# Trainium2, one core: first layernorm's halves abreast, bias shifts summed on VectorE first, norm steps timed by single matmuls, last image's MLP and convolution by token halves

## The chip, the cores and the metric

One NeuronCore of a Trainium2 chip runs the whole program in one launch. The metric is the device time in microseconds (us), the median over several executions. Times of stages come from one profiled execution of each kernel, whose span is about 2 us shorter than the timed median.

## The reference, cut to what matters

Eight images of 384 channels and 32 x 32 tokens pass a transformer block, then a ConvNeXt-like block. All arithmetic is fp32.

```python
# block 1, per image; C = 384, N = 1024 tokens, 8 heads of 48
xn = layernorm(x, g1, beta1)                       # eps 1e-5
q, k, v = xn @ w_qkv.T + b_qkv
x1 = softmax(q k^T * SCALE) v @ w_proj.T + b_proj + x
x2 = x1 + gelu(layernorm(x1, g2, beta2) @ w_fc1.T + b_fc1) @ w_fc2.T + b_fc2   # hidden 1536
# block 2, per image
y = depthwise_conv_7x7(x2) + dw_b                  # one filter per channel, padding 3
y = gelu(layernorm(y, ln_w, ln_b) @ w1 + b1)       # eps 1e-6, hidden 1536
gx = sqrt(sum over tokens of y^2);  nx = gx / (mean over hidden of gx + 1e-6)
y = (gamma * y * nx + gbeta + y) @ w2 + b2
out = x2 + y
```

Below, fc1 and fc2 are the two matmuls of block 1's MLP; the GRN (global response normalization) is the scaling by `nx` in block 2, with the up-projection `w1` before it and the down-projection `w2` after it. A norm's additive vector (`beta1`, `beta2`, `ln_b`, `gbeta`) is folded once into the bias of the matmul behind it: that is a bias shift. The kernel calls the last two shifts lnb and gbeta.

## The kernel before: the parts that the change touches

Activations lie with channels on the 128 partitions (3 channel tiles, `CT`) and tokens along the free dimension, in two halves of 512 (`NH`). TensorE multiplies; VectorE does the 7 x 7 convolution as 147 fused multiply-adds per image over a padded copy; ScalarE does exponentials and GELU; GpSimd does the layernorm's additions and copies rows into the padded image. While TensorE works on image b's attention and MLP, VectorE convolves image b-1.

In the traces each engine executes its instructions in the order in which the program emits them (in the changed kernel VectorE's first subtraction, whose sum was ready at 10.4 us, stands behind two additions and starts at 14.2), so the program decides where a layernorm's matmul stands among the MLP's matmuls. It does this with an emission clock: `flow.pe(us)` advances it by the TensorE time of what was just emitted, and background chains (generators) take their next step when the clock passes the delay that they yielded.

```python
U = 0.857                       # us of one 128x128 by 512 fp32 matmul

class Flow:
    def pe(self, us):           # TensorE work was emitted: step the chains that are due
        self.now += us
        ...
        while self.due and self.due[0][0] <= self.now:
            at, _, chain, paced = heapq.heappop(self.due)
            self._step(chain, at, paced)
    ...
def shift(dst, lhsT, name, nk, bias, rows=slice(0, P)):   # bias + W^T beta, one column
    ps = o_tile(f"shift_{name}")
    for k in range(nk):
        nc.tensor.matmul(out=ps[rows, :1], lhsT=lhsT(k), rhs=col(name, k), start=(k == 0), stop=(k == nk - 1))
    nc.vector.tensor_tensor(dst, ps[rows, :1], bias, ALU.add)

def linear_half(lhsT, rhs, nk, h, name):
    ps = o_tile(name)
    for k in range(nk):
        nc.tensor.matmul(out=ps, lhsT=lhsT(k), rhs=rhs(k)[:, half(h)], start=(k == 0), stop=(k == nk - 1))
    flow.pe(nk * U)             # the clock ticks once per tile
    return ps

def layernorm(src, dst, h, eps, g, name, switch):
    cols = half(h)
    a = one.tile([P, NH], F32, tag="ln_a", name=f"{name}_a{h}")
    nc.gpsimd.tensor_tensor(a, src[:, 0, cols], src[:, 1, cols], ALU.add)
    nc.gpsimd.tensor_tensor(a, a, src[:, 2, cols], ALU.add)
    yield 3.5
    total = o_tile(f"{name}_sum{h}")
    nc.tensor.matmul(out=total, lhsT=ones, rhs=a, start=True, stop=True)
    flow.pe(U)
    yield 1.0
    for ct in range(CT):        # x - mean
        nc.vector.scalar_tensor_tensor(dst[:, ct, cols], total, -1.0 / C, src[:, ct, cols], ALU.mult, ALU.add)
    yield 0.8
    ...                         # three squares on ScalarE, "yield 0.7" after each
    nc.gpsimd.tensor_tensor(squares[0], squares[0], squares[1], ALU.add)
    nc.gpsimd.tensor_tensor(squares[0], squares[0], squares[2], ALU.add)
    yield 3.5
    var = o_tile(f"{name}_var{h}")
    nc.tensor.matmul(out=var, lhsT=ones, rhs=squares[0], start=True, stop=True)
    flow.pe(U)
    yield 1.0
    ...                         # rstd = exp(-0.5 ln(var + eps)) on ScalarE
    yield 2.6 if switch else 1.2
    for ct in range(CT):
        nc.vector.scalar_tensor_tensor(dst[:, ct, cols], dst[:, ct, cols], col(g, ct), rstd, ALU.mult, ALU.mult)

def both(*args):                # one half after the other
    for h in range(2):
        yield from layernorm(*args[:2], h, *args[2:])

def mlp(b, xt, xn, weights, tag, ln, rest, before_fc2, fold):
    ...
    flow.finish(ln)             # the second norm, half 0
    for m in range(HT):         # fc1 on half 0: 12 tiles of 3 matmuls
        if fold and m + 2 < HT:
            fold_fc1(weights, wa, m + 2)          # a shift
        gelu_half(hid, m, 0, xn, weights, wa, bfc1, f"fc1_{b}")
        if m == 3 and rest:
            rest()              # second half of the output projection
            ln = flow.spawn(layernorm(xt, xn, 1, eps0, "g2", f"ln2_{b}", True))
    flow.finish(ln)             # whatever of half 1's norm is not emitted yet comes here
    for m in range(HT):
        gelu_half(hid, m, 1, xn, weights, wa, bfc1, f"fc1_{b}")
        weights.used(wa, m)
    if before_fc2:
        before_fc2()            # spawns the norms of the image before and the image after
    for ct in range(CT):        # fc2 on both halves, then x += ..., copied into the padded image
        ...

def convolution(acc, us):       # us: paced emission
    for i in range(KS * KS):
        dy, dx = divmod(i, KS)
        for ct in range(CT):
            window = pad[:, ct, dy : dy + H, dx : dx + W]
            dst = image(acc[:, ct, :])
            ...
            nc.vector.scalar_tensor_tensor(dst, window, tap, dst, ALU.mult, ALU.add)
            yield us

# main, end of the run
for b in range(B):
    ...
    mlp(b, xt, xn, weights, b, ln2, rest, norms, b == 0)
    ...
    if b == B - 1:
        start_conv(b, "xn", 1.3)                  # the last convolution: only after the last MLP
    y, gx = grn_up(b - 1, acc, weights, b - 1, b == 1)
    ...
    scale = flow.spawn(grn_scale(b - 1, gx, weights, b - 1, b == 1))
    next_values(b + 1)
    flow.finish(scale)
    grn_down(b - 1, y, kept.pop(b - 1), weights, b - 1, b - 1)
flow.finish(state["conv"])
acc = state["acc"]
flow.finish(both(acc, acc, eps1, "lnw", f"ln3_{B - 1}", True))
y, gx = grn_up(B - 1, acc, weights, B - 1, False)
...
```

## Time and profile before

| | before |
|---|---|
| time, median of the first 3 runs | 3819.84 us (3818.61 to 3821.57) |
| span of the profiled run | 3816.7 us |
| TensorE busy, idle | 3660.0 us, 157 us |
| first query matmul | 62.9 us |
| second output projection of the last image starts | 3325.1 us |
| from there to the end | 491.6 us |

TensorE's own time line at the start (start us, length us, engine, line, operation, out<-in, tile, count) shows what the first part of the change is after: 60 matmuls of one column each (120 records), for the bias shifts, stand between the first norm and the values.

```profile
25.28 2.07 PE L281 MATMUL ln_var<-ln_sq,ones 128*128 128x512 f32 x2 [5.59 <-POOL ln_sq L278]
27.15 10.24 PE L200 MATMUL shift_beta<-vec,wqk_sb 128*128 128x1 f32 x48
37.31 2.26 PE L200 MATMUL shift_beta<-vec,wv_sb 128*48 128x1 f32 x48
39.51 5.28 PE L652 MATMUL bout<-bv,wproj_sb 128*128 128x1 f32 x24
44.65 18.43 PE L319 MATMUL v<-wv_sb,xn 128*128 128x384 f32 x48
```

The bracket names what the engine waited for just before, 5.59 us for GpSimd's sum of squares. A record count is twice the number of matmuls that the program wrote.

### The profile page before, as it was taken

The page shows a single profiled execution, that of the slowest core. Times are in us where ns is not written, and L with a number is a line of the kernel's source. Part 1 is how long each engine was busy: PE and PEld are TensorE (multiplying, and loading weights), DVE is VectorE, ACT ScalarE, POOL GpSimd, SP SyncE. Part 2 cuts the span into 40 slices and gives each one's busy share as a digit, 9 for nine tenths or more (in the row PEclk, how much of TensorE's full clock was granted, in tenths as well). Part 3 has the DMA queues.
Part 4 walks back from the last instruction along what each step waited for, and adds up shares of the span by engine and source line. Part 5 has one row for each costly group of instructions (what it writes and reads, how often), then busy time and mean ns, then how long its engine had stood idle before and what let it go on. Part 6 is the DMA issues. An engine that isn't in the chain of part 4 may idle for free.

```text
span 3816.7 us, 36079 instructions
## 1 busy us (share of the span) xinstructions
PE 3660.0 (96%) x14882; PEld 1620.2 (42%) x14882; DVE 1862.4 (49%) x1931; ACT 1264.8 (33%) x1523; POOL 433.9 (11%) x294
## 2 busy tenths in 40 slices
PE   8999999999999999999999999999999999999658
PEld 4354444454444434444344443444444443444223
DVE  1011785246732668227571366524673256826930
ACT  1541352313523144240542415322352314423021
POOL 1011021200112002110021001120021200210010
PEclk9999999999999999999999999999999999999879
DMA  2002101201012200121002210021101210002100
GB/s 103 13 12 58 45 18 45 70 29 45 18 45 75 65 10 16 42 88 52 13 12 62 68 53 16 25 88 36 45 18 44 75 57 19 15 25 72 53 18 29
DMA packets 87148, 161.47 MB, mean 42 GB/s; under 512 B 25920, under 2 KB 26048, under 8 KB 86848
## 3 DMA queue, kind: packets, MB, share of 16 engines
q1 hardware_dynamic: 86400, 156.01, 13.6%
q8 instruction: 119, 1.95, 0.2%
q10 hardware_dynamic: 576, 3.07, 0.2%
q14 instruction: 53, 0.43, 0.0%
HBM read 133.36 MB, written 25.69 MB: 42 GB/s over the span
## 4 chain that ended last, share of the span: by engine, by line
PE 95%; DVE 2%; ACT 2%; POOL 1%; DMA 0%; issue 0%; DVEq 0%; SPq 0%; POOLq 0%; ACTq 0%
PE fc L250 13%; PE o L235 13%; PE h L235 13%; PE fc L235 13%; PE o L401 12%; PE s L381 11%; PE qk L235 9%; PE proj L333 4%; PE v L319 3%; DVE acc L538 2%; PE ln_sum L265 1%; PE ln_var L281 1%; ACT L255 1%; PE shift_beta L200 1%; PE shift_gbeta L200 0%; DMA xn<-in_x 0%
## 5 line engine op out<-in xcount | busy, mean ns | idle before, releaser
L538 DVE SCALAR_TENSOR_TENSOR acc<-pad,vec,acc 128x1024 f32<-128x1024 f32 x1152 | 1449.1, 1326 | 0.0
L390 ACT ACTIVATE p<-s 128x1024 f32<-128x1024 f32 x512 | 523.7, 1025 | 401.3 <-PE s L381 401.2
L381 PE MATMUL s<-qk 64*64 64x512 f32 x4096 | 563.1, 591 | 11.5 <-ACT p L390 10.0
L401 PE MATMUL o<-p,v 64*64 64x512 f32 x4096 | 560.9, 590 | 0.0
L250 PE MATMUL fc<-xn,fc 128*128 128x512 f32 x1152 | 515.7, 606 | 26.9 <-DVE xn L292 26.9
L235 PE MATMUL o<-y,w 128*128 128x512 f32 x1152 | 499.8, 596 | 3.2 <-issue 3.2
L235 PE MATMUL h<-acc,w 128*128 128x512 f32 x1152 | 502.3, 594 | 0.6 <-DVE acc L292 0.6
L235 PE MATMUL fc<-hid,fc 128*128 128x512 f32 x1152 | 502.4, 593 | 0.0
L250 PEld LDWEIGHTS fc<-xn,fc 128*128 128x128 f32 x1152 | 221.7, 194 | 310.5 <-issue 269.6
L235 PEld LDWEIGHTS o<-y,w 128*128 128x128 f32 x1152 | 220.2, 191 | 279.1 <-issue 273.3
L235 PEld LDWEIGHTS fc<-hid,fc 128*128 128x128 f32 x1152 | 219.2, 190 | 276.4 <-issue 276.4
L235 PEld LDWEIGHTS h<-acc,w 128*128 128x128 f32 x1152 | 218.2, 190 | 272.0 <-issue 269.4
L235 PE MATMUL qk<-xn,wqk_sb 128*128 128x512 f32 x768 | 330.9, 592 | 0.0
L368 POOL TENSOR_TENSOR attn<-attn,r 128x512 f32<-128x512 f32 x64 | 103.4, 1615 | 1897.2 <-DMA r<-back 1896.5
L381 PEld LDWEIGHTS s<-qk 64*64 64x64 f32 x4096 | 178.6, 133 | 279.3 <-issue 229.0
L401 PEld LDWEIGHTS o<-p,v 64*64 64x64 f32 x4096 | 185.3, 133 | 258.2 <-issue 252.6
L483 ACT ACTIVATE hid<-fc,bfc_f 128x512 f32<-128x512 f32 x192 | 132.0, 687 | 457.3 <-PE fc L250 457.3
L306 ACT ACTIVATE qk<-qk,bqk 128x1024 f32<-128x1024 f32 x64 | 71.3, 1114 | 634.2 <-PE qk L235 634.2
L350 DVE TENSOR_TENSOR attn<-o,attn 128x512 f32<-128x512 f32 x64 | 44.3, 691 | 396.5 <-ACT attn L348 396.1
L235 PEld LDWEIGHTS qk<-xn,wqk_sb 128*128 128x128 f32 x768 | 145.9, 190 | 183.3 <-issue 182.5
L552 ACT ACTIVATE y<-h,b_f 128x1024 f32<-128x1024 f32 x96 | 107.0, 1114 | 290.2 <-PE h L235 290.0
L269 DVE SCALAR_TENSOR_TENSOR acc<-ln_sum,acc 128x512 f32<-128x512 f32 x48 | 30.2, 684 | 283.7 <-PE ln_sum L265 283.7
(90 smaller groups left out, 1843.3 us busy)
## 6 DMA issues: line engine op xcount, KB each, us to landing
fc<-in_wfc SPq DMA_DIRECT2D x96, 384.0 KB
w<-in_w SPq DMA_DIRECT2D x96, 384.0 KB
r<-back SPq DMA_DIRECT2D x128, 128.0 KB
xn<-in_x SPq DMA_DIRECT2D x16, 768.0 KB
x<-in_x SPq DMA_DIRECT2D x16, 768.0 KB
kept<-x SPq DMA_DIRECT2D x8, 1536.0 KB
res<-kept SPq DMA_DIRECT2D x48, 256.0 KB
out_y<-res SPq DMA_DIRECT2D x48, 256.0 KB
```

The lines of the kernel that those rows point to most:

```text
L235: nc.tensor.matmul(out=ps[:, half(h)], lhsT=lhsT(k), rhs=rhs(k)[:, half(h)], start=(k == 0), stop=(k == nk - 1),)
L250: nc.tensor.matmul(out=ps, lhsT=lhsT(k), rhs=rhs(k)[:, half(h)], start=(k == 0), stop=(k == nk - 1))
L306: nc.scalar.activation(parts[:, i, :], ps, AF.Identity, bias=bqk[:, i : i + 1], scale=SCALE if i < NP else 1.0)
L319: nc.tensor.matmul(out=ps[:, :C], lhsT=xn[:, k, t * P : (t + 1) * P], rhs=wv_sb[:, k, :], start=(k == 0), stop=(k == CT - 1),)
L333: nc.tensor.matmul(out=ps, lhsT=wproj_sb[:, m, ct * P : (ct + 1) * P], rhs=attn[:, m, :], start=(m == 0), stop=(m == NP - 1),)
L368: nc.gpsimd.tensor_tensor(attn[:, m, :], attn[:, m, :], r, ALU.mult)
L381: nc.tensor.matmul(out=s[64 * i : 64 * i + 64, j, :], lhsT=kT[64 * j : 64 * j + 64, m, k0 : k0 + 64], rhs=qT[64 * j : 64 * j + 64, m, half ...
L390: nc.scalar.activation(p, s, AF.Exp)
L401: nc.tensor.matmul(out=outs[i][64 * j : 64 * j + 64, :], lhsT=v[keys, t, at : at + 64], rhs=p[keys, j, :], start=(t == 0), stop=(t == KT - 1),
L483: nc.scalar.activation(hid[:, m, half(h)], ps, AF.Gelu, bias=bias[:, m : m + 1])
L538: nc.vector.scalar_tensor_tensor(dst, window, tap, dst, ALU.mult, ALU.add)
L552: nc.scalar.activation(y[:, m, :], ps, AF.Gelu, bias=b1[:, m : m + 1])
```

## The change

Its intent is to fill three kinds of TensorE's idle time. (1) At the start, the norm's two halves run abreast (half 1 with VectorE in GpSimd's place), and a bias shift `W^T beta` is formed as a weighted sum of the weight's tiles on VectorE and then one matmul with a column of ones, instead of one matmul for each tile; most of the shifts move into the first attention. (2) The emission clock ticks after each matmul of a half and the norm's yields are shorter, so that norm steps stand earlier in TensorE's order. (3) The last image's MLP runs token half by token half, so that VectorE can start the first 13 rows of the last convolution after half 0, and the last norm runs abreast.

```diff
-    def shift(dst, lhsT, name, nk, bias, rows=slice(0, P)):
-        ...
+    def weighted(dst, parts, name):
+        for k, part in enumerate(parts):
+            if k == 0:
+                nc.vector.tensor_scalar(dst, part, col(name, 0), None, ALU.mult)
+            else:
+                nc.vector.scalar_tensor_tensor(dst, part, col(name, k), dst, ALU.mult, ALU.add)
+
+    def column_sums(ps, i, weights, rows=slice(0, P)):
+        nc.tensor.matmul(out=ps[rows, i : i + 1], lhsT=weights, rhs=ones[:, 0:1], start=True, stop=True)
+        flow.pe(0.2)
     ...
     def linear_half(...):
         for k in range(nk):
             nc.tensor.matmul(...)
-        flow.pe(nk * U)
+            flow.pe(U)
+            if done:
+                done(k)
     ...
-    def layernorm(src, dst, h, eps, g, name, switch):
+    def layernorm(src, dst, h, eps, g, name, switch, spare=False):
         ...                       # spare: VectorE adds, buffers from the attention's ring
-        yield 3.5                 # after the adds          (+ 3.2)
-        yield 1.0                 # after the sum matmul    (+ 0.8)
-            yield 0.7             # after each of 3 squares (+ one 1.8 after all three)
-        yield 3.5                 # after the square adds   (+ 3.0)
-        yield 1.0                 # after the var matmul    (+ 0.8)
+    def abreast(*args):           # both halves in lockstep, half 1 with spare=True
+        chains = [layernorm(*args[:2], h, *args[2:], spare=(h == 1)) for h in range(2)]
+        ...
+    def mlp_by_halves(b, xt, xn, weights, ln, rest, between):
+        for h in range(2):
+            ...                   # fc1 on half h; its weights are loaded for each half
+            if h == 0:
+                between(-1)       # spawns the norm of the image before
+            for ct in range(CT):
+                ps = linear_half(... fc2 on half h ...)
+                nc.vector.scalar_tensor_tensor(dst, ps, col("bfc2", ct), dst, ALU.add, ALU.add)
+                nc.gpsimd.tensor_copy(inner(ct)[:, rows, :], dst...)
+            between(h)            # spawns convolution rows 0:13, then 13:32
     ...
     def grn_up(b, acc, weights, tag, fold):
         ...
+        if fold:
+            t = two.tile([P, NH], F32, tag="r", name="w2_gbeta")[:, :C]
+            weighted(t, [weights.at(wb, k) for k in range(HT)], "gbeta")
+            sum_ = o_tile("b2")
+            for ct in range(CT):
+                column_sums(sum_, ct, t[:, ct * P : (ct + 1) * P])
     ...
     def main():
-        flow.finish(both(xn, xn, eps0, "g1", "ln1_0", False))    # in effect
+        flow.finish(abreast(xn, xn, eps0, "g1", "ln1_0", False))
     ...
-            if b == B - 1:
-                start_conv(b, "xn", 1.3)
+            else:
+                norm3 = flow.spawn(after(state["conv"], abreast(last, last, eps1, "lnw", f"ln3_{b}", True)))
```

`last` is the query/key weight's buffer, which is free by then and takes the last convolution's result. Two pieces are not in the cut: the second-last image's convolution is emitted at 1.65 us a step and not 1.9, and some memsets and loads at the start stand elsewhere.

## The prediction

> **What bounds the kernel now.** I read the page's totals first, then the waits of TensorE, then the chain that ended last and the time line of the start and the end. The totals, then two rows of the 40 slices:
>
> ```profile
> PE 3660.0 (96%) x14882; PEld 1620.2 (42%) x14882; DVE 1862.4 (49%) x1931; ACT 1264.8 (33%) x1523; POOL 433.9 (11%) x294
> ...
> PE   8999999999999999999999999999999999999658
> ...
> PEclk9999999999999999999999999999999999999879
> ```
>
> TensorE (PE) is the bound for all but 157 us (3816.7 - 3660.0), and the two dips are the first slice and the last three. A change can pay only by filling PE's idle time, by removing matmuls, or by keeping its clock up. Who PE waited for, in all:
>
> ```profile
> PE ln_sum L265 <- POOL ln_a L262: 79.1, 6, 66.1
> PE fc L250 <- DVE xn L292: 26.9, 8, 3.4
> PE ln_var L281 <- POOL ln_sq L278: 21.1, 4, 6.0
> PE s L381 <- ACT p L390: 10.0, 8, 1.2
> PE gxsum L562 <- ACT gx L559: 7.8, 2, 3.9
> ```
>
> Columns: total us, times, longest. The reader sees one wait of 66.1 us, and one of 3.4 us that comes once an image. The chain of work that ended last, in the last 300 us, shows what the 66.1 is (start, length):
>
> ```profile
> 3527.23 64.27 PE o L235 x144
> ...
> 3592.93 60.99 DVE acc L538 x51
> ...
> 3679.08 61.22 PE h L235 x142
> ```
>
> The last image's convolution (147 VectorE instructions over 1024 elements) starts only after its MLP, lies beside 128 us of the image before's GRN matmuls, and sticks out; then its layernorm runs bare, half after half. PE stands from 3591.5 to 3679.1. VectorE by shape (count, busy us, mean ns):
>
> ```profile
> L538 DVE SCALAR_TENSOR_TENSOR acc<-pad,vec,acc 128x1024 f32<-128x1024 f32 x1152 | 1449.1, 1326 | 0.0
> L583 DVE TENSOR_SCALAR w<-w,gscale 128x384 f32<-128x384 f32 x96 | 32.4, 416 | 0.2
> ```
>
> At the end, undisturbed, 52 of the first kind take 62.27 us: 1.20 us from one to the next. At the start, per the time line, layernorm ends some 31 us in, tiny matmuls (the folded shifts) fill PE from 27.2 to 44.7, values start at 44.65, queries at 62.91.
>
> **What the Trainium skill says.**
> - "TensorE: Matmul & The Clock Gate", section "What's actually happening": the array's clock halves after about 3.4 us idle and comes back after about 3.4 us of busy. The trace agrees: after each 3.4 us wait of line 250 the next 72 records take 32.73 us, against 72 x 0.429 = 30.9 in steady flow, so a wait costs 3.36 + 1.85 = 5.2 us. The 17 us of one-column matmuls at the start leave it cold: the first eight value records come 0.64 us apart, later 0.32.
> - "VectorE: DVE Perf Modes", section "The TRN2 errata": a fixed cost per instruction, (N + 151)/0.96 ns for an fp32 tensor_tensor. Here the adds of 512 elements (line 350) take 691 ns, which is exact; 1024 elements of the fused form take 1228 at the least (formula 1224). Cutting a convolution in two pays the fixed part twice.
> - "ScalarE: Activation LUTs", section "What ACT_TABLE_LOAD costs": 1283 ns a load. The trace has 1.28 us.
>
> **The change, part by part.**
>
> 1. *Start.* Both halves of the first layernorm go abreast: half 0 sums on GpSimd, half 1 on VectorE. From the trace: data of half 0 at 5.5, sum matmul to 10.3, subtraction, squares, GpSimd adds to about 16, variance to 18.1, rstd 1.4 us, scaling: half 0 is ready near 21 (half 1 about 2 us later, and only the fifth value tile needs it). Values start at 21 instead of 44.65 and last the same 18.4 us (they start cold in both). The query/key shift, 48 records before, is now 16 behind the values: 3 us. Queries start at 42.3 instead of 62.9: **-20.6**.
> The other shifts move into the first attention, where PE is the bound: value shift 16 records x 0.05, fc1 shift 24 x 0.16, output bias 24 x 0.16 (0.16 from the 72 records of the gbeta shift in 11.7 us): about 9 us, and 2 for a clock that may fall during them: **+11**. The fc1 shifts vanish from the first MLP: starts of successive fc1 tiles lie 3.24 us apart instead of 2.68, 12 x 0.56: **-6.6**. The lnb shifts go from 72 records to 24 (12 x 0.67 before, about a third after): **-5**. The gbeta shift held PE 11.1 us; now PE waits for 12 dependent VectorE instructions over 384 elements, which nothing covers: 11 x 0.64 + 0.45 = 7.5, plus ends, about 9: **-2**.
>
> 2. *Layernorm's timing.* The emission clock ticks after each matmul in a half, not after three, and the yields are shorter. Listing the order of the instructions: the variance matmul of the second norm's half 1 stood behind the twelfth fc1 tile of half 0; now it stands in the ninth, 11 matmuls (9.4 us) before half 1 begins. From variance to the first scaled tile takes 2 to 5 us, so the 3.4 us wait and its cold clock go, in images 0 to 6: 7 x 5.2 = **-36.6** (image 7 is in part 3). The same shortening puts sum and variance earlier in the attention, where GpSimd, slowed by the convolution on VectorE (2.2 us an add there, 1.26 alone), was done only 0.6 us before its sum matmul: I give back 1 us in each of 7 images, **+7**, and 1.7 where the second image's load is late anyway (a 3.3 us wait today).
>
> 3. *End.* The last MLP runs half by half (its weights load twice), so the convolution starts after fc2 of half 0. PE leaves half 0 of fc1 at 3357.9. fc2 half 0 is 36 x 0.857 = 30.9, with four norm matmuls 3.4: 3392.2. VectorE starts at 3393. Spacing is 0.133 + 1.043 ns an element (from 1.201 at 1024 and 0.667 at 512): 0.567 us at 416 elements, 0.766 at 608. First piece 83 us, second 112, so 195 against 177 unsplit. In VectorE's order there are three fc2 adds (2.0) in the first piece, then 56 of the second, the GRN scale (5), 91 more and six output adds (4). End: 3393 + 195 + 11 = **3599**, against 3655 before. PE meanwhile: fc1 and fc2 of half 1 to 3454, GRN up to 3516, scale, GRN down 3522 to 3586. VectorE reaches the scale at 3520.5, when the sum is ready at 3520.3, so it does not hold PE. After the convolution the abreast norm: GpSimd adds 3.5, two cold sum matmuls, subtraction, squares, adds, two variance matmuls, rstd with a second table load in between, first scaled tile of half 1: about 17 us, against 24. PE starts the last GRN at 3616 instead of 3679: **-63**. The 137.6 us after that do not change.
>
> Sum: -20.6 + 11 - 6.6 - 5 - 2 - 36.6 + 7 + 1.7 - 63 = -114. 3819.8 - 114 = **3706 us**, 3.0% less.
>
> **Rivals.**
> - *VectorE's lag becomes a wait of PE.* In the last image VectorE has 206 us of work in an unbroken row, and the GRN scale waits in that row. If instructions of 416 elements cost 0.08 us more than I reckon (a fixed cost misjudged, or GpSimd's copies to the padded image slowing them), the scale comes 12 us late and the norm 20: gain at the end 43 and not 63, time 3726. For: the mean over the run is 1326 ns, not 1228. Against: GpSimd has nearly nothing to do in that stretch.
> - *The earlier norm matmuls block PE.* PE is in order; a sum or variance matmul whose GpSimd half is not done stops everything behind it. 48 norm halves, each 1 us late, would eat the 36.6: time 3735. For: slack of only 0.6 us in the attention. Against: elsewhere sum to variance has 10.3 us of emission for about 6 us of work, and only two such waits in the middle of the run exist today.
> - *DMA.* The doubled weights add 4.7 MB, 12 loads of 384 KB. The queue is busy 14%; a ring of 9 tiles puts each load some 24 us ahead of its use. I expect nothing from it.
> - *Better than reckoned:* if the attention hides the extra waits, 3695.
>
> **Range and chances.** The end is the largest term and its error perhaps 10 us, mostly to the bad side; the 36.6 comes from a listed order and a repeated wait and may lose 10 more; the start is good to 6. 8 in 10: 3684 to 3730. For less than 2% gain the time would have to be above about 3745, which needs both bad rivals at once.
>
> **What the new profile would show.** Step 1: values' first matmul near 21 us, queries near 42; if half 1 lands late, sum of half 1 waits for DMA. A wait of PE for the gbeta column of VectorE of 7 to 8 us. Step 2: the row of PE waiting for the norm's scaling (3.4 us, 8 times) gone, and 72 records of fc1 half 1 in 30.9 us; new small waits at sum and variance in the attention, about 1 us an image. Step 3: the 66 us wait down to some 15 to 20, convolution ending 55 us earlier relative to fc1 of the last image, instruction spacing 0.57 and 0.77 us. It would be wrong if PE waits for the GRN scale or a weight load in the last image, or if norm matmuls show waits in the middle images that sum to tens of us.

## The result

The changed kernel takes 3702.36 us (median of 4 runs, 3700.94 to 3704.35); the kernel before took 3819.44 us in the same rounds. The ratio is 0.9693, with a 95% interval of 0.9676 to 0.971. Ratios here are the mean time of one kernel's runs over that of the other's of the same rounds, so not quite the ratio of the medians quoted.

The totals and two rows of the 40 slices of the changed kernel:

```profile
PE 3620.0 (98%) x14656; PEld 1531.7 (41%) x14656; DVE 1910.0 (52%) x2151; ACT 1260.3 (34%) x1517; POOL 460.8 (12%) x296
...
PE   8999999999999999999999999999999999999978
...
PEclk9999999999999999999999999999999999999989
```

TensorE's idle time fell from 157 us to 82 (3701.6 - 3620.0), and its busy time by 40 us: fewer one-column matmuls, and fewer matmuls run at a cold clock (the mean granted clock is 0.990, against 0.982). The dip to 5 and 6 tenths in the last slices is gone. TensorE's waits by what ended them (total us, times, longest):

```profile
PE ln_sum L281 <- POOL ln_a L278: 33.4, 16, 15.3
...
PE b L206 <- DVE w_gbeta L202: 7.8, 1, 7.8
PE ln_var L296 <- POOL ln_sq L293: 5.6, 2, 3.1
PE ln_sum L281 <- DVE ln_t L278: 3.9, 1, 3.9
```

The 66.1 us wait became 15.3. The eight waits of 3.4 us for the norm's scaling are gone. New are many short waits at norm sums (16 where there were 6) and one of 7.8 us for the gbeta column. The chain of waits at the start (start, length):

```profile
1.25 11.56 DMA xn<-in_x
...
14.17 0.69 DVE xn L285
...
23.16 17.79 PE v L349 x48
40.95 1.68 PE bqk L206 x16
```

And at the end:

```profile
3426.89 40.41 DVE wqk_sb L589 x53
...
3472.38 18.37 DVE wqk_sb L589 x25
...
3545.10 2.35 POOL ln_a L277
...
3562.39 63.46 PE h L243 x142
```

The convolution ends at 3545.1 and TensorE's unbroken run of the last up-projection starts 17.3 us later (its first matmul alone, 2 records, stands before it, at 3559.7). "Start of the last up-projection" means this run below, and the last norm's time is counted up to it. VectorE's instructions of the two pieces, by shape (busy us, mean ns):

```profile
L589 DVE SCALAR_TENSOR_TENSOR wqk_sb<-pad,vec,wqk_sb 128x608 f32<-128x608 f32 x144 | 110.2, 842 | 0.0
L589 DVE SCALAR_TENSOR_TENSOR wqk_sb<-pad,vec,wqk_sb 128x416 f32<-128x416 f32 x144 | 81.3, 645 | 0.0
```

By stage, from the time lines of the two kernels:

| stage | before, us | after, us | difference | predicted |
|---|---|---|---|---|
| to the first query matmul | 62.9 | 42.5 | -20.4 | -20.6 |
| on to the first output projection | 112.0 | 123.1 | +11.1 | +11 |
| on to the last image's second projection | 3150.2 | 3105.0 | -45.2 | -41.5 (fc1 -6.6, lnb -5, gbeta -2, timing -36.6 + 7 + 1.7) |
| on to the end | 491.6 | 431.0 | -60.6 | -63 |

There was a surprise in GpSimd's time line of the last image. Three copies of half 0 into the padded image take 0.62 us each (the first line is the last of them); three copies of half 1, which lie beside VectorE's unbroken row of convolution instructions, take 11 to 18 us:

```profile
3339.69 0.62 POOL L569 COPY pad<-x 128x512 f32<-128x512 f32 x1 [7.90 <-DVE x L567]
3383.81 11.11 POOL L569 COPY pad<-x 128x512 f32<-128x512 f32 x1 [43.50 <-DVE x L567]
3395.16 11.67 POOL L569 COPY pad<-x 128x512 f32<-128x512 f32 x1 [0.24 <-DVE x L567]
3407.07 17.86 POOL L569 COPY pad<-x 128x512 f32<-128x512 f32 x1 [0.24 <-DVE x L567]
```

The first two end within 0.6 us after VectorE began its next fc2 addition, an instruction with one input in PSUM and one in SBUF (3394.4, 3406.3), the third just after VectorE began the second piece's opening multiplications, which have one SBUF input (3424.4). The Trainium skill, "SBUF — State Buffer", section "Who interferes with whom", says that a VectorE instruction with two SBUF inputs contends with a GpSimd instruction that reads SBUF, and each convolution step has two. Here nothing waited for these copies. Whether they matter is tested below.

### The profile page after: what moved, and what is told of

It reads as the page before. It is cut to its first block, busy times and chain, and to the rows that moved or that the text cites. A ratio compares the mean times of both kernels' runs of the same rounds, so it can differ in the third digit from the quotient of the medians.

```text
span 3701.6 us, 35866 instructions
## 1 busy us (share of the span) xinstructions
PE 3620.0 (98%) x14656; PEld 1531.7 (41%) x14656; DVE 1910.0 (52%) x2151; ACT 1260.3 (34%) x1517; POOL 460.8 (12%) x296
## 3 DMA queue, kind: packets, MB, share of 16 engines
q1 hardware_dynamic: 88128, 160.73, 14.4%
## 4 chain that ended last, share of the span: by engine, by line
PE 90%; DVE 7%; POOL 1%; ACT 1%; DMA 1%; issue 0%; SPq 0%; DVEq 0%; POOLq 0%
PE fc L258 13%; PE h L243 12%; PE o L243 12%; PE o L431 12%; PE fc L243 12%; PE s L411 11%; PE qk L243 9%; DVE wqk_sb L589 5%; PE proj L363 4%; PE v L349 3%; PE ln_sum L281 1%; PE ln_var L296 1%; POOL ln_a L278 1%; DVE acc L589 1%; DMA xn<-in_x 0%; ACT L265 0%
## 5 line engine op out<-in xcount | busy, mean ns | idle before, releaser
L589 DVE SCALAR_TENSOR_TENSOR acc<-pad,vec,acc 128x1024 f32<-128x1024 f32 x1008 | 1280.0, 1334 | 0.0
L411 PE MATMUL s<-qk 64*64 64x512 f32 x4096 | 534.6, 592 | 11.5 <-ACT p L420 10.0
L431 PE MATMUL o<-p,v 64*64 64x512 f32 x4096 | 529.8, 590 | 0.0
L243 PE MATMUL fc<-hid,fc 128*128 128x512 f32 x1008 | 442.6, 594 | 0.0
L243 PE MATMUL h<-acc,w 128*128 128x512 f32 x1008 | 437.2, 593 | 0.0
L243 PEld LDWEIGHTS fc<-hid,fc 128*128 128x128 f32 x1008 | 192.3, 191 | 242.5 <-issue 242.5
L243 PEld LDWEIGHTS h<-acc,w 128*128 128x128 f32 x1008 | 190.7, 190 | 235.8 <-issue 235.8
L411 PEld LDWEIGHTS s<-qk 64*64 64x64 f32 x4096 | 152.3, 133 | 305.2 <-issue 261.9
L431 PEld LDWEIGHTS o<-p,v 64*64 64x64 f32 x4096 | 155.5, 133 | 286.0 <-issue 282.8
L589 DVE SCALAR_TENSOR_TENSOR wqk_sb<-pad,vec,wqk_sb 128x416 f32<-128x416 f32 (+1 forms) x288 | 191.5, 744 | 0.0
```

The costliest lines, as they stand in the source:

```text
L243: nc.tensor.matmul(out=ps[:, half(h)], lhsT=lhsT(k), rhs=rhs(k)[:, half(h)], start=(k == 0), stop=(k == nk - 1),)
L411: nc.tensor.matmul(out=s[64 * i : 64 * i + 64, j, :], lhsT=kT[64 * j : 64 * j + 64, m, k0 : k0 + 64], rhs=qT[64 * j : 64 * j + 64, m, half ...
L431: nc.tensor.matmul(out=outs[i][64 * j : 64 * j + 64, :], lhsT=v[keys, t, at : at + 64], rhs=p[keys, j, :], start=(t == 0), stop=(t == KT - 1),
```

## The experiments

The theory is that the three parts do what the prediction says, each on its own: the start and the shifts 23 us, the timing by removing a wait and the cold clock behind it, the end by VectorE's row starting and ending earlier. The main rival is that they are not independent. All ratios are to the kernel before. The first four runs take the parts one by one.

### Part 1 alone

The changed kernel with the old clock ticks, yields and end:

```diff
-            flow.pe(U)                        # in linear_half
+        flow.pe(nk * U)
-        yield 3.2 ... 0.8 ... 1.8 ... 3.0 ... 0.8
+        yield 3.5 ... 1.0 ... 0.7 x 3 ... 3.5 ... 1.0
-            mlp_by_halves(...)                # last image, and the last norm abreast
+            mlp(...)                          # as before, and both(...)
```

> Part 1 alone (first norm abreast, shifts summed on VectorE first), the timing of the norms and the end of the run as before. Theory: the parts are independent; the start gives -20.4 (queries from 62.9 to 42.5 us), the shifts in the first attention cost +8.8, fc1 shifts -6.6, lnb shifts -6.5, gbeta -2: about -27 us, 3793 us, ratio 0.993, with the 3.4 us wait before half 1 of fc1 still there eight times. Rival (the start only moves the wait to the attention): less than 10 us.

Measured: 3799.05 us, ratio 0.9947 (0.9931 to 0.9964), 21 us less. That lies 6 us short of what I wrote for this run, and 2 us short of the prediction's own sum (-23.2). The time line tells why. Queries start at 43.0 us, not 42.5. The first attention became 11.1 us longer, not 8.8: in the changed kernel's trace the shift matmuls themselves take 8.8 us, and the three groups of 8 attention records behind them start 1.8, 1.7 and 1.2 us apart where later ones are 0.86 apart, 2.1 us more, as the prediction had allowed for the clock. The fc1 shifts gave 6.4 net: half 0 of fc1 became 8.0 us shorter, but the 72 records after image 0's wait took 32.8 us where they had taken 31.2. The lnb shifts gave 5.5: a tile's shift had added 0.67 us, its column sum adds 0.22. The gbeta part gave nothing. In the changed kernel TensorE's wait of 7.8 us, 1.4 us of column sums, and 2.3 us because the next 12 value records took 6.40 us against 4.12 (the run with gbeta moved, below, has those) are 11.5, as long as the 11.3 us of matmuls that they replaced; in this run the 12 records took 7.11.

### Part 2, whole and by pieces

Part 2 alone, on the kernel before:

```diff
-        flow.pe(nk * U)
+            flow.pe(U)
-        yield 3.5 ... 1.0 ... 0.7 x 3 ... 3.5 ... 1.0
+        yield 3.2 ... 0.8 ... 1.8 ... 3.0 ... 0.8
```

> Part 2 alone: the emission clock ticks at each matmul of a half and the norm's yields are shorter; start and end as before. Theory: 8 x 5.2 = 41 us gained (all eight images here), 4 to 7 given back in waits at sum and variance matmuls: -34 to -37 us, 3783 to 3786 us, ratio 0.9905; the row of PE waiting for the norm's scaling is gone. Rival 1 (earlier norm matmuls block PE): waits at sum and variance of over 15 us, time above 3795. Rival 2 (the clock after the wait was not cold because of it): the gain is 8 x 3.4 = 27 less 5, 3797 us.

Measured: 3786.21 us, ratio 0.9911 (0.9895 to 0.9928), -34 us, as the theory has it. The second piece alone, only the tick:

```diff
-        flow.pe(nk * U)
+            flow.pe(U)
```

> The tick at each matmul alone, with the old longer yields. In the listed order the variance matmul of the second norm's half 1 then lies 8 matmuls (6.9 us) ahead of half 1 of fc1, against 0 before and 11 with the whole of part 2. Theory: the wait needs only its 3.4 us covered, so the tick alone gives the whole 41 us, and without the shorter yields nothing is given back: 3778 us, ratio 0.989, a few us better than both together. Rival (the shorter yields are what works): above 3800.

Measured: 3778.51 us, ratio 0.9892 (0.9875 to 0.9908), -42 us against 41 expected. The wait for the norm's scaling is absent from the waits of both. Their first rows are, for part 2 whole and then for the tick alone:

```profile
PE ln_sum L265 <- POOL ln_a L262: 85.8, 19, 66.1
```

```profile
PE ln_sum L265 <- POOL ln_a L262: 79.4, 6, 66.1
```

The tick alone has the kernel before's 6 waits at norm sums; with the shorter yields there are 13 more, 6.4 us in sum. The period of an image in the middle of the run, from one GRN sum to the next, is 454.1 us before, 448.8 with the tick and 449.4 with both. So the wait costs 5.3 us an image, clock included, and the shorter yields cost 0.6.

### Part 3 alone

Only the last image by halves and the last norm abreast, with the old ticks and yields, on the kernel before:

```diff
-            mlp(b, xt, xn, weights, b, ln2, rest, norms, b == 0)
+            if b < B - 1:
+                mlp(...)
+            else:
+                mlp_by_halves(...)            # and conv in two pieces, last norm abreast
```

> Part 3 alone (last image's MLP and convolution by token halves, last norm abreast), start and timing as before. Theory: from the end of fc1's half 0 of the last image to the end the changed kernel took 397.3 us against 458.8, so -61 us, 3758 us, ratio 0.984; a wait of TensorE for the last norm of 15 us and not 66. Rival (the end's gain needs parts 1 and 2 to be had): above 3775.

Measured: 3778.21 us, ratio 0.9889 (0.9872 to 0.9905): -42 us, not -61. The rival was right: 20 us of the end's gain need another part. TensorE's waits show a new one of 15.6 us at a variance matmul:

```profile
PE ln_var L288 <- POOL ln_sq L285: 31.0, 4, 15.6
```

GpSimd's time line of this run (the columns as above) says what ended it:

```profile
3445.65 11.67 POOL L569 COPY pad<-x 128x512 f32<-128x512 f32 x1 [44.90 <-DVE x L567]
3457.55 11.11 POOL L569 COPY pad<-x 128x512 f32<-128x512 f32 x1 [0.24 <-DVE x L567]
3468.63 1.26 POOL L284 TENSOR_TENSOR ln_sq<-ln_sq,ln_sq 128x512 f32<-128x512 f32 x1
3469.96 1.26 POOL L285 TENSOR_TENSOR ln_sq<-ln_sq,ln_sq 128x512 f32<-128x512 f32 x1
```

These adds belong to the norm of the image before. Their squares were ready at 3431.4, but in GpSimd's order they stand behind two of the long copies. In the changed kernel that norm is emitted within fc2 of half 0 and is done before VectorE's row begins; with the old tick, once in 12 matmuls (10.3 us) in fc2, it drags on into the row.

### What was missing in part 3 alone

The first test gives part 3 only the tick, and only in the last image's fc2:

```diff
+            if each:                          # each=True for fc2 of the last image alone
+                flow.pe(U)
```

> Part 3 with one piece of part 2: the emission clock ticks at each matmul in the fc2 halves of the last image only. In part 3 alone the norm of the image before advanced only once per 12 matmuls (10.3 us) there, so its second half fell into VectorE's unbroken convolution row, its GpSimd adds queued behind the locked copies, and TensorE waited 15.6 us at a variance matmul. Theory: with the tick the norm is done before the row begins, the 15.6 us wait goes, and the end is worth its 61 us: 3758 to 3761 us, ratio 0.984. Rival (what was missing in part 3 alone lies in the other images' timing or in the start): no change, 3778 us.

Measured: 3765.41 us, ratio 0.9857 (0.9842 to 0.9872), 55 us less than before; the 15.6 us wait is gone (the longest at a variance is 5.6, at the start). So the order of that norm is 13 us of the 20. From the last image's second projection to the end it takes 436.6 us, against 450.4 in part 3 alone and 431.0 in the changed kernel. Of the 5.6 us that remain, 1.9 are in the convolution, which ends 276.4 us after the second projection and not 274.5: the last scaling of the norm of the image before, 2.1 us, still falls into VectorE's row:

```profile
3404.98 2.07 DVE L303 SCALAR_TENSOR_TENSOR acc<-acc,vec,ln_rstd 128x512 f32<-128x512 f32 x3
```

Another 2.6 are in the last norm (19.9 us and not 17.3: with a yield after each square the lockstep interleaves the squares of the two halves on ScalarE), and 1.2 in the last GRN (140.4 against 139.2). There is also a wait before the second-last GRN's down-projection, 4.7 us where the changed kernel has at most 1.9: VectorE came 3.2 us later to the scale, with that scaling and two more convolution steps in front of it. That is the prediction's first rival, in small. It is not time lost at the end by itself, since TensorE waits another 14.4 us for the last norm afterwards.

The second test leaves the order and lets GpSimd in:

```diff
+                if y1 < H and (i * CT + ct) % 4 == 3:
+                    nc.vector.tensor_scalar(pause, eps1, 1.0, None, ALU.mult)   # one column
```

> Part 3 alone again, with a VectorE instruction of one column and one SBUF input after every fourth instruction of the first piece of the last convolution (36 of them), nothing else. Theory (GpSimd cannot read SBUF while VectorE runs instructions with two SBUF inputs back to back, and gets in only at an instruction with one): each of the locked copies, 11 to 12 us in part 3 alone, takes at most 4 x 0.567 + 0.7 = 3 us, the 15.6 us wait of TensorE falls below 4 us, VectorE's idle 6 us goes; the pauses cost 36 x 0.1 to 0.2 us; time 3762 to 3768 us. Rival (GpSimd only shares bandwidth with VectorE): the copies keep over 8 us each and the time gets worse by the pauses, 3783 us.

Measured: 3779.82 us, ratio 0.9892 (0.9877 to 0.9907), no better than without. The copies are short now, as the theory said:

```profile
3448.95 0.98 POOL L570 COPY pad<-x 128x512 f32<-128x512 f32 x1 [45.99 <-DVE x L568]
3461.54 0.98 POOL L570 COPY pad<-x 128x512 f32<-128x512 f32 x1 [11.60 <-DVE x L568]
3462.49 1.59 POOL L285 TENSOR_TENSOR ln_sq<-ln_sq,ln_sq 128x512 f32<-128x512 f32 x1
```

GpSimd's additions get in too, and then it is VectorE that pays: the four steps beside a copy and two additions took 4.7 us, where four steps otherwise take 2.3:

```profile
3461.39 4.71 DVE L590 SCALAR_TENSOR_TENSOR wqk_sb<-pad,vec,wqk_sb 128x416 f32<-128x416 f32 x4
```

But the time did not follow, and the waits say why: the variance wait halved and another took its place.

```profile
PE ln_var L289 <- POOL ln_sq L286: 23.3, 4, 7.9
...
PE h L236 <- DVE acc L301: 6.7, 1, 6.7
```

The second copy still starts only at 3461.5, because the fc2 addition that feeds it stands that far back in VectorE's own row, and the norm's scaling stands behind the third addition, which VectorE reaches at 3474.7. So the copies are shut out and not merely slowed: pauses of 0.06 us brought them from 11 us to 1 (the last one to 3). (The pause is short and has one SBUF input; which of the two lets GpSimd in was not separated.) Yet what cost the time is the order: a norm emitted into the row is held by VectorE's order with or without the lock. My theory had put the whole 15.6 us down to the lock; that part of it fell.

### Old yields in the changed kernel

```diff
-        yield 3.2 ... 0.8 ... 1.8 ... 3.0 ... 0.8
+        yield 3.5 ... 1.0 ... 0.7 x 3 ... 3.5 ... 1.0
```

> The changed kernel with the old, longer yields of the norm; the tick at each matmul stays. Theory: the small norm waits of 0.6 us an image go (seven of them, 4 us); at the end the last three scaling instructions of the norm fall behind the start of VectorE's row and cost 0 to 3 us: 3698 to 3702 us, no worse than the changed kernel. Rival (the shorter yields are needed, in the middle or at the end): above 3710.

Measured: 3701.41 us, ratio 0.9691 (0.9678 to 0.9705), the same as the changed kernel. The middle gains (period 448.8 us) and the end loses 3.1 us (434.1 against 431.0), in the places just seen: the convolution ends 1.2 us later, again with 2.1 us of the norm's scaling in its row, the last norm takes 19.9 us, and the last GRN is 0.6 us shorter. The wait before the second-last down-projection, 4.8 us, is there too. The shorter yields thus help only at the end; the tick is the part that works.

### One piece instead of two, and the last norm in turn

The changed kernel with the last convolution in one piece:

```diff
-            rows = (split, H) if h else (0, split)
+            if h == 0:
+                return
+            rows = (0, H)
```

> The changed kernel with the last convolution in one piece, started after the second half of the MLP; the MLP stays in halves and the norm abreast. Theory: VectorE's row starts at about 3401 us (end of fc2's half 1) instead of 3339.5, 62 us later, and is 147 x 1.201 + 4 (GRN scale) + 4 (output adds) = 185 us long instead of 205: it ends 41 us later, and TensorE's wait at the last norm's sum grows by as much: 3743 us. Rival (the row is hidden, TensorE is the bound there): within 10 us of 3702.

Measured: 3754.49 us, ratio 0.9828 (0.9812 to 0.9845), 52 us more than the changed kernel. The row is on the path, as the theory says; it is 11 us longer than reckoned because VectorE ran ahead of the paced emission and stood still for the GRN scale, here in its time line:

```profile
3401.95 52.70 DVE L589 SCALAR_TENSOR_TENSOR wqk_sb<-pad,vec,wqk_sb 128x1024 f32<-128x1024 f32 x44
3464.90 0.17 DVE L629 TENSOR_REDUCE gmean<-gxsum 128x1 f32<-128x12 f32 x1 [10.26 <-PE gxsum L626]
```

The last norm in turn:

```diff
-after(state["conv"], abreast(last, last, ...
+after(state["conv"], both(last, last, ...
```

> The changed kernel with the last norm's halves one after the other, as the kernel before had it. Theory: the time from the end of the convolution to the first matmul of the last up-projection goes from 17.4 back to 24 us: plus 6.6, 3709 us, and TensorE's two waits there together 6 to 7 us longer. Rival (half 1's work on VectorE is in the way of half 0, so abreast gains nothing): within 2 us of 3702.

Measured: 3711.92 us, ratio 0.9715 (0.9702 to 0.9729), 9.6 us more than the changed kernel's median of another job. In its trace the convolution ends at the same 3545.1, and the last up-projection starts at 3569.8 and not 3562.4: 7.4 us, near the 6.6 expected; the span's other 1.7 us lie in the last GRN (140.9 against 139.2).

### The start and the gbeta wait

wv and wqk behind the image's halves on the same queue:

```diff
-        nc.scalar.dma_start(out=wv_sb, in_=...)
-        load_wqk()
+        nc.sync.dma_start(out=wv_sb, in_=...)
+        load_wqk(nc.sync)
```

> The changed kernel with the loads of wv and wqk put behind the image's two halves on the same DMA queue, instead of beside them on another. Theory: half 1 of the first image landed only at 12.8 us because those loads shared the engines with it, and VectorE, in order, kept half 0's subtraction waiting for half 1's adds until 14.2 us although its sum was ready at 10.4. With the image first, half 1 lands near 9 us, the subtraction starts near 10.6, values at 19.7 us instead of 23.2, queries 3 us earlier: 3699 us. Rival (VectorE's order is not what held half 0, or wqk then comes too late for its weighting): queries not earlier than 42 us.

Measured: 3700.21 us, ratio 0.9685 (0.9671 to 0.9698); the median is only 2 us lower, which these rounds do not separate, but the trace is plain. VectorE's first two groups of the start, half 1's additions and then the subtractions:

```profile
7.49 1.17 DVE L277 TENSOR_TENSOR ln_t<-xn 128x512 f32<-128x512 f32 x1 [7.49 <-DMA xn<-in_x]
...
10.28 3.68 DVE L285 SCALAR_TENSOR_TENSOR xn<-ln_sum,xn 128x512 f32<-128x512 f32 x6 [0.89 <-PE ln_sum L281]
```

Half 1 lands at 7.5 us and not 12.8, half 0's subtraction starts at 10.3 and not 14.2, values at 19.3 and not 23.2, queries 3.4 us earlier.

The gbeta weighting beside the up-projection:

```diff
+            for k in [2 * (m - 6), 2 * (m - 6) + 1]:     # inside the loop over m
+                if fold and 0 <= k < HT:
+                    ...                                  # one of the 12 weighted additions
-            weighted(t, [weights.at(wb, k) for k in range(HT)], "gbeta")
```

> The changed kernel with the weighting of w2 by GRN's beta (12 dependent VectorE instructions) spread beside the last six up-projection tiles instead of after them. Theory: TensorE's wait of 7.8 us and the half clock after it (12 value records in 6.3 us against 3.9) go, nothing is added to TensorE: 10 us less, 3692 us. Rival (the wait only moves to the weight loads or to the lnb sums): within 3 us of 3702.

Measured: 3693.9 us, ratio 0.9669 (0.9656 to 0.9682), 8.5 us less than the changed kernel. A wait of 1.4 us remains, since the last two additions come after the last tile:

```profile
PE b L206 <- DVE attn L617: 1.4, 1, 1.4
```

### A version that beats both

The four edits together: gbeta beside the up-projection (one tile earlier than above), the image first on its queue, old yields except in the last norms, and the GRN scale of the second-last image on ScalarE:

```diff
+            if b == B - 2:
+                nc.scalar.mul(w, w, scale[:, m : m + 1])
+            else:
                 nc.vector.tensor_scalar(w, w, scale[:, m : m + 1], None, ALU.mult)
```

> A version meant to beat both: the changed kernel with (a) the gbeta weighting beside the up-projection, (b) the image first on the DMA queue, (c) the old yields in the norms except the last image's and the last two, (d) the GRN scale of the second-last image on ScalarE instead of in VectorE's row (12 instructions, 4 us). Theory, term by term from the traces: -10 - 3.3 - 4.2 - 4 = -21: 3681 us; TensorE's gbeta wait under 0.3 us, no row of small norm waits in images 1 to 6, VectorE's last row 201 us instead of 205. Rival (VectorE's row is not what ends that stage): the end keeps its length and the time is 3685.

Measured: 3681.69 us (3679.46 to 3682.93), ratio 0.9639 (0.9625 to 0.9652), 21 us below the changed kernel. The sum is as expected, the terms are not quite. At the first projection it is 4.6 us ahead of the changed kernel, from gbeta it gains 10.8, the yields and the rest bring it to 22.0 by the GRN sum of the second-last image. From there to the end it takes 235.3 us, exactly as the changed kernel does: the scale on ScalarE gave nothing. VectorE's time line shows where the freed 4 us went, into a wait for TensorE's down-projection in the middle of the row:

```profile
3446.23 20.68 DVE L592 SCALAR_TENSOR_TENSOR wqk_sb<-pad,vec,wqk_sb 128x608 f32<-128x608 f32 x27
3470.81 1.41 DVE L667 SCALAR_TENSOR_TENSOR res<-o,b_f,res 128x512 f32<-128x512 f32 x2 [3.91 <-PE o L243]
```

In program order 27 convolution steps stand between the scale and the first output addition, and VectorE, 4 us earlier, met an addition whose operand was not there.

## Why the prediction was right, point by point

The time, 3702.4 us, lies 4 us from the 3706 predicted, inside the range.

- **Start.** The step held (-20.4 against -20.6), by errors that cancel and by luck. Values start at 23.2 us and not 21: the prediction took half 1's arrival as harmless to half 0, but half 1 landed at 12.8 us and VectorE's in-order additions for it held half 0's subtraction for 3.7 us, as the queue experiment shows. Against that, the query/key sums took 1.7 us and not 3, and the values 17.8 and not 18.4. The last of these varies: in the traces of two variants with the same start (gbeta moved, one piece) the values took 15.8 us and the queries start at 40.5, so this step is good to 2 us and no better.
- **Shifts.** The first attention grew by 11.1 us against 11. The fc1 term was under-sized: tiles without a shift start 2.57 us apart (6 records of 0.429), not 2.68, so half 0 became 8.0 us shorter and not 6.6; part 1 alone kept 6.4 of it. The lnb term was right (5.5 against 5, with the column sum a third of the shift, as reckoned). The gbeta term was over-sized (0 against 2): 7.8 us of wait was foreseen as 7.5, but the cold clock after it was left out.
- **Timing.** The wait's cost of 5.2 us an image is confirmed by the tick alone (5.3). Its reading was loose, though: "after each wait" the 72 records took 31.2 us in image 0, 33.9 in image 1 and 32.7 to 32.9 in the others, and the same 72 without a wait before them take 31.1 in the changed kernel (its 30.9 leaves out the end of the last record), so the slow clock usually costs 1.7 us and not 1.85. The second image's late load made TensorE wait 5.1 us instead of 3.3, as foreseen (1.7 more). The give-back was over-sized: 0.6 us an image and not 1. The mechanism given for it, norm matmuls standing before GpSimd is done, is what the 13 extra short waits show. The prediction did not see that the yields were unneeded for the gain.
- **End.** -60.6 against -63. The convolution row took 205.4 us against 206 (3599 - 3393), with instruction spacings of 0.562 and 0.763 us against 0.567 and 0.766, and the norm 17.3 against 17 (before, it took 25.0 us from 3654.1 on, not 24 from 3655). The last GRN took 1.6 us longer than before (139.2 us against 137.6), which had been taken as unchanged; its first 142 records took 63.5 us against 61.2.
- **Rivals.** VectorE did reach the scale in time in the changed kernel (3467.2, when the sum's matmul had ended 0.3 us before), but only just: two variants show TensorE waiting 4.7 to 4.8 us there. "GpSimd has nearly nothing to do in that stretch" was wrong as an argument: its three copies took 41 us, and part 3 alone shows norm work caught there. The second rival, norm matmuls that block TensorE, came in small: 13 waits, 6.4 us in sum, in part 2 alone. Of the DMA rival nothing is seen: no wait of TensorE in the changed kernel's trace is for a weight load.
- **Not seen at all.** The prediction added the parts as if they were independent. Alone they give 21, 34 and 42 us, in sum 97; together 117. The missing 20 us are part 3's, and it gets 13 of them back by the finer tick in the last image's fc2 alone. The total came out right because the prediction's chain for part 3 used the norm positions of the whole change.

## What to carry to other kernels

Where engines are in order, emit small cross-engine chains finely enough that each step stands between single matmuls, and before any long unbroken row of another engine that shares their work. A change of several parts is best priced in the order in which it will stand, since a part's gain can depend on another part's order. Time freed in the middle of a row that meets a producer soon after (the GRN scale moved to ScalarE) is only turned into a wait.

## What the Trainium skill lacked or had wrong

- "SBUF — State Buffer", section "Who interferes with whom", has a GpSimd instruction that reads SBUF block against a VectorE instruction with two SBUF inputs, one instruction against one. It does not say what a row does: GpSimd copies of 512 elements were not let in between 19 to 31 back-to-back VectorE instructions of that kind, and took 11.1 to 17.9 us against 0.62 alone. One VectorE instruction of one column and one SBUF input after every fourth let them through in 0.98 us (2.97 for the last), for about 0.06 us each (four steps and a pause take 2.31 us from start to start, four steps 2.25). Nor does it tell copies from additions: in part 3 alone, GpSimd's additions of two tiles beside the same kind of row took 1.48 to 1.61 us (1.26 alone), where the copies took over 11. It was VectorE that waited there: with the pauses in, four steps beside a copy and two additions took 4.71 us, against 2.33. What sets copies and additions apart was not tested.
- "VectorE: DVE Perf Modes", section "The TRN2 errata", gives (N + 151)/0.96 ns for one fp32 tensor_tensor. The section has no figure for the spacing of fused multiply-adds in an unbroken row, which the prediction took from the trace: here 0.562 us from start to start at 416 elements and 0.763 at 608, where that formula, which is for the duration of one instruction, has 0.591 and 0.791.
